# A four-layer graph network on one core: a reordered opening with dummy transposes, and a sign change moved from ScalarE to GpSimd

## The chip, the cores and the metric

The kernel runs on one core of a Trainium2 chip. The core has a matrix engine (TensorE, PE in the profile, with its weight loads shown apart as PEld), a vector engine (VectorE, DVE), a scalar engine (ScalarE, ACT), a general engine (GpSimd, POOL) and a queue engine that only starts transfers (SyncE, SP). Each engine works through its own instructions strictly in order; semaphores tie them together. The metric is the time of one execution on the device in microseconds; lower is better. Most repeats of this kernel agree within a few tenths of a per cent, with an occasional one above.

## What is computed

`x` holds 32 graphs of 512 nodes with 128 features; `adj` is one symmetric 0/1 matrix of 512x512 with a full diagonal, shared by all graphs. Four layers follow each other, each wrapped in a residual sum and a layer norm:

```python
x = _layernorm(x + _L0_gnn_ref(x, adj, W, b, a_src, a_dst))   # graph attention, leaky relu
x = _layernorm(x + _L1_gnn_ref(x, adj, W, a_src, a_dst))      # graph attention, elu
x = _layernorm(x + _L2_gnn_ref(x, adj, W, e, bias))           # weights by edge, diagonal apart
x = _layernorm(x + _L3_gnn_ref(x, adj, weight, bias))         # adj @ x + x, linear, L2 norm
# attention (layers 0 and 1):
h = x @ W;  e_src = h @ a_src;  e_dst = h @ a_dst
alpha = softmax(leaky_relu(e_src[:, None] + e_dst[None, :], 0.2) + mask(adj))
out = alpha @ h
# layer norm:
(x - mean(x)) / sqrt(var(x) + 1e-5)
```

All is float32. With these inputs all values of `e` are equal, so layer 2 is a mean over neighbours; the kernel tests that and two other properties of the inputs on the device and has a general path for when they fail. That path is not run here.

## The kernel before

Everything is unrolled. A graph's work is cut into named units ("pt0", "al0", "nrm2" and so on), each a few instructions on one engine, and a table gives every unit of every graph its place in one long list: `PLAN[name][graph]` for the work of the graphs, `STARTS[name]` for work done once. The list is sorted by these numbers and emitted in that order (L613 to L632), with buffers taken from fixed stocks when a unit first names a tile and returned after its last use. So the order on each engine is written out by hand (by an offline planner), nothing is scheduled at build time, and several graphs are always in flight.

Units of one graph in attention layer k (0 or 1): "ld" starts the transfer of x (L142, on SP); "pt" makes four 128x128 transposes (L149, PE), "xt" copies them out (L153, ACT); "pha/phb" multiply by the weight matrix extended by three attention columns (L167, PE); "exa/exb" take exponentials of those three columns (L171, ACT) into the array `exps`; "ha/hb" scale the projected features (L177, ACT), "pc" puts the scale in a last column (L192, POOL); "pr" spreads one exponential along a row by four transposes (L197, PE); "al" builds the unnormalised attention matrix with the mask `mt` in four instructions of 128x512 (L205, DVE); "poa/pob" multiply it with the features (L184, PE, 16 matmuls, 32 records in the profile). Then come division and bias (L188, L212, L217), activation, residual ("add", L235, POOL), "bn" statistics (L307, L309, DVE), and the norm. The statistics tile already carries epsilon. "ms" negates the mean (L313, ACT), "pw" takes the power -1/2 of the variance and multiplies the negated mean by it (L317, L318, POOL), and "nrm" applies scale and shift (L323, ACT). Layers 2 and 3 split x into two parts ("xh" L241 ACT, "xl" L245 POOL) for exact products with a 512x512 matrix (L252, PE), copy out (L256), and multiply by weights (L266, L267, L279); layer 3 has a row norm (L289 ACT, L293 and L294 POOL, L300 DVE). "st" writes the result (L328, SP).

Work done once. `first()` (L334) issues on the ACT queue the layer-0 weights W0, its two attention vectors, a quarter of `adj`, and the same three transfers of layer 1; on SP the other three quarters of `adj`; it builds the identity (POOL), fills constants, and clears the eight statistics tiles. In the list, six "ld" come first (places 0 to 5), then six "pt0"/"xt0", then "awt0" (the transpose of W0, L364, PE), "awc0" (its copy, L368, DVE), "e0" to "e3" (threshold of the four pieces of `adj`, L385, DVE), "awq0" and "aws0" (attention columns, L372 and L377 to L379), "am" (mask transposes, L390, PE), "m" (mask copies, L395 DVE and L397 ACT), "rest" (seven constant transfers, L358, SP), "deg" (node degrees, L412 and L413, DVE), "cva/cvd" (the matrices of layers 2 and 3, L401, L402 ACT and L407, L408 POOL), and the three input tests "lpp/lpd" (L418, L422), "dv" (L427, L428) and "de" (L432 to L434).

Of the kernel before, what the change touches and what calls it, by code (L numbers as in the profile page):

```python
# [18 lines left out]
P = 128  # L19
Q = 32  # L20
EPS = 1e-5
# [4 lines left out]
def kernel(  # L26
# [48 lines left out]
    an, em = square("an"), square("em")  # L75
    mt = square("mt")
# [9 lines left out]
    exps = const.tile([P, B * 2, NCH, 3], F32, name="exps")  # L86
# [34 lines left out]
    kind("sq", 30, "x1 x2 x3 x4 o0 o1 o2 o3 t t3 xb y2 y3 xt0 xt1 xt2 tr1 tr2", plain([P, N]))  # L121
# [4 lines left out]
    kind("st", 8, "st0 st1 st2 st3", plain([P, NCH, 9]))  # L126
# [28 lines left out]
    def columns(xt, c, blocked):  # L155

        if blocked:
            return xt.rearrange("p (a c i) -> p c a i", a=4, c=NCH)[:, c]
        return xt[:, c * P : (c + 1) * P]

    for k in range(2):
        for half, s in enumerate("ab"):

            @unit(f"ph{k}{s}", f"xt{k}", f"ph{k}{s}")
            def _(b, xt, p, k=k, half=half):
                for c in range(2):
                    nc.tensor.matmul(twos(p)[:, c, :FE], columns(xt, 2 * half + c, (b, f"td{k}") in planned), ATT[k], start=True, stop=True)  # L167

            @unit(f"ex{k}{s}", f"ph{k}{s}")
            def _(b, p, k=k, half=half):  # L170
                nc.scalar.activation(pair(exps[:, 2 * b + k], half), twos(p)[:, :, F:FE], AF.Exp)  # L171

            @unit(f"h{k}{s}", f"ph{k}{s}", f"h{k}")
            def _(b, p, h, k=k, half=half):
                for c in range(2):
                    pc = exps[:, 2 * b + k, 2 * half + c, 1:2]
                    nc.scalar.activation(h[:, 2 * half + c, :F], twos(p)[:, c, :F], AF.Identity, bias=pc if k else 0.0, scale=pc)  # L177
# [12 lines left out]
        @unit(f"pc{k}", f"h{k}")  # L190
        def _(b, h, k=k):
            nc.gpsimd.tensor_copy(h[:, :, F], exps[:, 2 * b + k, :, 1])  # L192

        @unit(f"pr{k}", f"pr{k}")
        def _(b, p, k=k):
            for c in range(NCH):
                nc.tensor.transpose(p[:, c * P : (c + 1) * P], exps[:, 2 * b + k, c, 0:1].to_broadcast([P, P]), ident)  # L197

        @unit(f"al{k}", f"pr{k}", f"al{k}")
        def _(b, p, al, k=k):  # L200
            attention(b, k, p, al)

    def attention(b, k, r, al):
        for j in range(NCH):
            nc.vector.scalar_tensor_tensor(al[:, j, :], r, exps[:, 2 * b + k, j, 2:3], mt[:, j, :], op0=ALU.max, op1=ALU.mult)  # L205
# [57 lines left out]
    def _(b, y, xt, p):  # L263
        for c in range(NCH):
            cols = slice(c * P, (c + 1) * P)
            nc.tensor.matmul(p[:, cols], y[:, cols], w21, start=True, stop=False)  # L266
            nc.tensor.matmul(p[:, cols], columns(xt, c, (b, "td2") in planned), w20, start=False, stop=True)  # L267
# [34 lines left out]
    for k in range(4):  # L302
# [8 lines left out]
        @unit(f"ms{k}", f"mv{k}")  # L311
        def _(b, mv):
            nc.scalar.activation(mv[:, :, 0], mv[:, :, 0], AF.Copy, scale=-1.0)  # L313

        @unit(f"pw{k}", f"mv{k}", f"rn{k}")
        def _(b, mv, rn):
            nc.gpsimd.tensor_tensor(rn[:, 0], mv[:, :, 1], mhalf, op=ALU.pow)  # L317
            nc.gpsimd.tensor_mul(rn[:, 1], mv[:, :, 0], rn[:, 0])  # L318

# [10 lines left out]
    for n in ("aw0", "aw1", "aq0", "aq1", "pm0", "pm1", "pm2", "pm3", "pflag"):  # L330
        KIND[n] = "ps"
    KIND["loops"], KIND["other"] = "sq", "al"

    def first():  # L334
        def attention_weights(k, w, a_src, a_dst):
            nc.scalar.dma_start(ATT[k][:, :F], w)
            for i, s in enumerate((a_src, a_dst)):
                nc.scalar.dma_start(acols[k][:, i : i + 1], bass.AP(tensor=s.tensor, offset=s.offset, ap=[[1, F], [1, 1]]))

        attention_weights(0, w0, asrc0, adst0)  # L340
        for c in range(NCH):
            (nc.scalar if c == 3 else nc.sync).dma_start(an[:, c, :], adj[c * P : (c + 1) * P, :])
# [4 lines left out]
        attention_weights(1, w1, asrc1, adst1)  # L347
        nc.gpsimd.tensor_scalar(nident, ident, -1.0, 1.0, op0=ALU.mult, op1=ALU.add)
        nc.gpsimd.memset(ones, 1.0)
        for st in FREE["st"]:  # L350
            nc.gpsimd.memset(st[:, :, 6:8], 0.0)
            nc.gpsimd.memset(st[:, :, 8], P * EPS)

# [55 lines left out]

    @unit("deg")  # L410
    def _(b):
        nc.vector.tensor_reduce(rdeg, em, axis=AX.X, op=ALU.add)  # L412
# [13 lines left out]
    def _(b, other):  # L426
        nc.vector.tensor_tensor(other, an, em, op=ALU.not_equal)  # L427
        nc.vector.tensor_reduce(doubts[:, 1:2], other.rearrange("p c f -> p (c f)"), axis=AX.X, op=ALU.max)  # L428
# [8 lines left out]
    def _(b):  # L437
        flat = exps.rearrange("p n c e -> p (n c e)")
# [12 lines left out]
    def _(b, p):  # L451
# [3 lines left out]
        "awt0": 13, "awc0": 16, "e0": 17, "rest": 19, "awq0": 21, "am0": 22, "e1": 24, "aws0": 25, "e2": 26,  # L455
        "awt1": 27, "am1": 28, "awc1": 29, "e3": 30, "deg": 32, "lpp": 33, "am2": 34, "am3": 37, "lpd": 42, "m2": 43,
        "awq1": 44, "m1": 46, "m0": 47, "cva2": 49, "m3": 50, "aws1": 52, "cva3": 55, "cvd2": 57, "cva0": 59,
        "cvd3": 60, "cva1": 61, "cvd0": 62, "dv": 63, "cvd1": 66, "de": 85, "out_d": 2297, "out_p": 2366,
        "out_c": 2370,
    }  # L460
    PLAN = {
        "ld": [5, 131, 168, 232, 184, 261, 1, 3, 4, 0, 2, 304, 298, 345, 513, 539, 787, 383, 665, 829, 904, 957, 1216,
            1245, 1067, 1349, 1154, 1578, 1434, 1696, 1791, 1819],
        "pt0": [18, 134, 169, 233, 195, 262, 7, 11, 15, 6, 9, 328, 422, 577, 624, 699, 793, 855, 799, 975, 1043, 959,
            1223, 1367, 1394, 1483, 1540, 1579, 1631, 1698, 1793, 1820],
        "xt0": [23, 136, 175, 235, 198, 266, 10, 14, 20, 8, 12, 340, 429, 582, 626, 704, 797, 866, 804, 985, 1052, 962,
            1229, 1371, 1400, 1491, 1543, 1586, 1637, 1705, 1797, 1829],
        "ph0a": [36, 140, 179, 241, 206, 270, 48, 56, 93, 65, 101, 350, 514, 597, 645, 731, 803, 872, 969, 990, 1090,
            1187, 1234, 1449, 1450, 1497, 1551, 1593, 1643, 1711, 1802, 1834],
        "ph0b": [31, 139, 182, 265, 203, 272, 45, 58, 91, 53, 51, 352, 523, 598, 641, 753, 805, 896, 973, 1031, 1113,  # L470
            1190, 1253, 1463, 1401, 1494, 1547, 1629, 1641, 1755, 1827, 1895],
        "ex0a": [38, 144, 185, 246, 208, 273, 67, 68, 96, 69, 104, 353, 518, 602, 650, 735, 806, 874, 974, 996, 1095,
            1192, 1246, 1454, 1452, 1503, 1554, 1600, 1651, 1718, 1805, 1837],
        "ex0b": [35, 141, 188, 269, 209, 281, 71, 73, 94, 74, 72, 361, 526, 603, 647, 766, 809, 900, 976, 1035, 1119,
            1199, 1257, 1468, 1410, 1505, 1552, 1639, 1644, 1765, 1831, 1900],
        "pc0": [39, 145, 190, 274, 211, 285, 75, 76, 98, 78, 105, 373, 531, 611, 652, 770, 815, 901, 979, 1042, 1122,
            1203, 1263, 1471, 1457, 1507, 1561, 1645, 1668, 1784, 1833, 1904],
        "pr0": [41, 146, 197, 276, 214, 290, 87, 90, 97, 95, 137, 399, 579, 655, 678, 772, 856, 922, 1029, 1099, 1158,
            1241, 1303, 1473, 1486, 1707, 1836, 1871, 1759, 1824, 1898, 1990],
        "h0a": [40, 148, 191, 279, 216, 287, 77, 79, 99, 83, 107, 384, 534, 616, 654, 774, 817, 905, 982, 1045, 1123,  # L480
            1205, 1267, 1479, 1462, 1509, 1562, 1647, 1669, 1785, 1835, 1905],
        "h0b": [64, 153, 194, 282, 218, 291, 80, 82, 100, 86, 108, 390, 537, 622, 660, 783, 820, 910, 986, 1050, 1127,
            1211, 1273, 1482, 1464, 1514, 1569, 1653, 1673, 1787, 1841, 1906],
        "al0": [54, 150, 213, 296, 230, 317, 92, 106, 113, 133, 200, 492, 583, 675, 769, 790, 869, 955, 1063, 1120,
            1188, 1282, 1315, 1650, 1516, 1714, 1866, 1903, 1762, 1826, 1921, 1996],
        "po0a": [81, 160, 222, 305, 248, 335, 103, 111, 126, 152, 215, 509, 620, 717, 782, 860, 907, 1008, 1075, 1147,
            1202, 1293, 1369, 1661, 1523, 1741, 1883, 1912, 1776, 1873, 1955, 2009],
        "po0b": [70, 163, 229, 313, 255, 342, 109, 115, 117, 207, 474, 499, 628, 737, 789, 865, 925, 1033, 1118, 1182,
            1212, 1314, 1387, 1667, 1533, 1732, 1877, 1917, 1783, 1902, 1970, 2056],
        "rs0a": [88, 164, 236, 316, 257, 364, 112, 123, 170, 172, 224, 515, 629, 722, 792, 868, 916, 1014, 1086, 1155,  # L490
            1222, 1299, 1377, 1670, 1531, 1752, 1891, 1920, 1788, 1879, 1971, 2022],
        "rs0b": [84, 171, 237, 332, 275, 357, 118, 122, 132, 228, 482, 508, 642, 759, 801, 878, 942, 1048, 1128, 1197,
            1221, 1325, 1398, 1679, 1548, 1739, 1885, 1928, 1799, 1909, 1979, 2069],
        "v0a": [89, 166, 245, 333, 283, 365, 119, 125, 173, 181, 226, 516, 637, 724, 796, 883, 923, 1015, 1088, 1162,
            1226, 1302, 1379, 1678, 1532, 1753, 1894, 1929, 1800, 1882, 1974, 2030],
# [454 lines left out]
```

## Time and profile before

| | us |
|---|---|
| median of three runs | 612.37 |
| lowest, highest | 612.05, 615.69 |
| the profiled execution | 614.38 |
| its span (first to last instruction in the profile) | 612.5 |
| first matmul record on PE starts at | 7.84 |
| PE, mean granted clock over the span | 0.985 |
| ACT, L313 (128x4), 128 times | 25.9 busy, 0.206 each |
| POOL, L317 / L318 (128x4), 128 times each | 1.042 / 0.212 each |
| POOL, L293 (128x4), 32 times | 0.228 each |
| DVE, L205 (128x512), 256 times | 173.4 busy, 0.738 each |
| ACT, L323 (128x128), 512 times | 209.4 busy, 0.488 each |

In the profile, a line such as "L184 PE MATMUL ps<-hp,al" names the source line, the engine, the operation and the tiles written and read. The instructions of an engine overlap a little, so the step from one to the next is shorter than the mean duration of one. A float32 matmul leaves two records on PE, a transpose one. "Idle before" is the time an engine stood still ahead of an instruction, with what ended it.

### The profile page before, as it was taken

What the parts mean: (1) busy time and instruction counts of PE and PEld (TensorE: products, weight loads), DVE (VectorE), ACT (ScalarE), POOL (GpSimd) and SP (SyncE); (2) the same over time, 40 slices, a digit from 0 to 9 for tenths busy, and PEclk for the clock granted to TensorE, in tenths of its full rate; (3) what the DMA queues carried; (4) which work ended last, traced back from release to release, by engine and by line L of the source; (5) the groups of instructions that cost most, each with busy time, mean ns of one, the idle gap of its engine ahead of it and who ended that gap; (6) DMA issues with size and microseconds to landing.
All of it is one profiled execution on the core that took longest, in us unless ns stands there. A gap on an engine that the chain in (4) does not pass through costs nothing.

```text
span 612.5 us, 13814 instructions
## 1 busy us (share of the span) xinstructions
PE 576.7 (94%) x4504; PEld 545.4 (89%) x4504; DVE 529.7 (86%) x1985; ACT 488.1 (80%) x1547; POOL 422.8 (69%) x580
## 2 busy tenths in 40 slices
PE   4898999999998999999999999999999999999881
PEld 4798998999998999989999999999999999998770
DVE  1998999787989999779989888799999999887864
ACT  3634777868889788786897989888885798999896
POOL 1422477586678776686768775868755786899885
PEclk9899999999999999999999999999999999999995
DMA  7001111000100111010201110010100001001003
GB/s 208 7 24 32 35 53 36 2 1 19 36 19 14 40 53 53 1 36 2 71 1 36 35 54 2 18 36 19 53 18 19 2 1 36 27 9 36 19 17 90
DMA packets 36316, 19.41 MB, mean 32 GB/s; under 512 B 1808, under 2 KB 35728, under 8 KB 36240
## 3 DMA queue, kind: packets, MB, share of 16 engines
q1 hardware_dynamic: 35232, 18.09, 10.3%
q8 instruction: 37, 0.61, 0.4%
q10 hardware_dynamic: 1008, 0.40, 0.2%
q14 instruction: 39, 0.32, 0.2%
HBM read 10.09 MB, written 8.39 MB: 30 GB/s over the span
## 4 chain that ended last, share of the span: by engine, by line
PE 68%; DVE 14%; ACT 8%; POOL 7%; issue 2%; DMA 1%; ACTq 0%; POOLq 0%; DVEq 0%
PE ps L184 30%; PE ps L252 12%; PE ps L167 8%; PE ps L149 5%; DVE al L205 5%; ACT sq L323 4%; PE ps L266 4%; PE ps L267 4%; PE ps L197 3%; PE ps L279 3%; DVE st L307 2%; POOL rn L317 2%; DVE sq L300 2%; POOL ss L294 1%; DVE sq L273 1%
## 5 line engine op out<-in xcount | busy, mean ns | idle before, releaser
L184 PE MATMUL ps<-hp,al 128*128 128x129 f32 x2048 | 246.1, 276 | 1.4 <-DVE al L205 1.1
L184 PEld LDWEIGHTS ps<-hp,al 128*128 128x128 f32 x2048 | 238.9, 192 | 3.7 <-DVE al L205 1.7
L323 ACT ACTIVATE sq<-sq,rn 128x128 f32<-128x128 f32 x512 | 209.4, 488 | 17.8 <-POOL rn L318 17.4
L205 DVE SCALAR_TENSOR_TENSOR al<-ps,exps,mt 128x512 f32<-128x512 f32 x256 | 173.4, 738 | 2.6 <-PE ps L197 2.5
L317 POOL TENSOR_TENSOR rn<-mv,mhalf 128x4 f32<-128x4 f32 x128 | 133.3, 1042 | 28.7 <-DVE mv L309 25.7
L307 DVE BATCH_NORM_STATS2 st<-sq 128x6 f32<-128x128 f32 x512 | 109.9, 276 | 12.4 <-POOL sq L235 12.3
L245 POOL TENSOR_TENSOR xr<-sq,xr 128x512 fp32r<-128x512 f32 x64 | 84.4, 1321 | 18.8 <-ACT xr L241 11.7
L177 ACT ACTIVATE hp<-ps,exps 128x128 f32<-128x128 f32 x256 | 89.3, 420 | 0.1
L153 ACT COPY sq<-ps 128x512 f32<-128x512 f32 x96 | 54.9, 582 | 28.6 <-PE ps L149 28.3
L167 PE MATMUL ps<-we,sq 128*128 128x131 f32 x512 | 71.5, 278 | 4.0 <-DVE al L205 2.5
L167 PEld LDWEIGHTS ps<-we,sq 128*128 128x128 f32 x512 | 64.2, 190 | 6.5 <-DVE al L205 2.7
L252 PE MATMUL ps<-off,xr 128*128 128x512 f32 x256 | 67.3, 405 | 1.1 <-DVE al L205 1.1
L252 PE MATMUL ps<-a3t,xr 128*128 128x512 f32 x256 | 66.6, 403 | 0.0
L235 POOL TENSOR_TENSOR sq<-sq,x 128x512 f32<-128x512 f32 x32 | 41.8, 1305 | 25.6 <-DVE sq L221 22.4
L260 POOL TENSOR_TENSOR sq<-sq,bias_b 128x512 f32<-128x512 f32 x32 | 41.0, 1283 | 21.2 <-ACT sq L323 19.2
L252 PEld LDWEIGHTS ps<-a3t,xr 128*128 128x128 f32 x256 | 46.3, 188 | 10.2 <-POOL xr L245 0.7
L252 PEld LDWEIGHTS ps<-off,xr 128*128 128x128 f32 x256 | 45.8, 188 | 10.3 <-DVE al L205 1.4
L266 PE MATMUL ps<-w,sq 128*128 128x128 f32 x256 | 49.8, 276 | 1.9 <-DVE al L205 1.8
L235 POOL TENSOR_TENSOR sq<-sq,sq 128x512 f32<-128x512 f32 x32 | 41.9, 1310 | 13.8 <-DVE rs L188 7.1
L267 PE MATMUL ps<-w,sq 128*128 128x128 f32 x256 | 49.5, 275 | 0.0
L313 ACT ACTIVATE mv<-mv 128x4 f32<-128x4 f32 x128 | 25.9, 206 | 29.3 <-DVE mv L309 21.2
L300 DVE SCALAR_TENSOR_TENSOR sq<-sq,ss,sq 128x128 f32<-128x128 f32 x128 | 42.3, 391 | 8.1 <-POOL ss L294 7.9
(78 smaller groups left out, 861.1 us busy)
## 6 DMA issues: line engine op xcount, KB each, us to landing
x<-in_x_dram SPq DMA_DIRECT2D x32, 256.0 KB, 2.9
out_dram<-sq SPq DMA_DIRECT2D x32, 256.0 KB, 2.2
an<-in_adj_dram SPq DMA_DIRECT2D x3, 256.0 KB, 3.9
an<-in_adj_dram ACTq DMA_DIRECT2D x1, 256.0 KB, 4.6
we<-in_L_gnn_W_dram ACTq DMA_DIRECT2D x2, 64.0 KB, 3.7
w<-in_L_gnn_W_dram SPq DMA_DIRECT2D x2, 64.0 KB, 3.4
bias_b<-in_L_gnn_bias_dram SPq DMA_DIRECT2D x2, 64.0 KB, 4.0
eb<-in_L_gnn_e_dram SPq DMA_DIRECT2D x1, 128.0 KB, 5.3
```

Source lines behind the costliest of these rows:

```text
L167: nc.tensor.matmul(twos(p)[:, c, :FE], columns(xt, 2 * half + c, (b, f"td{k}") in planned), ATT[k], start=True, stop=True)
L177: nc.scalar.activation(h[:, 2 * half + c, :F], twos(p)[:, c, :F], AF.Identity, bias=pc if k else 0.0, scale=pc)
L184: nc.tensor.matmul(twos(p)[:, c, : F + 1], al[:, j, rows], h[:, j, :], start=(j == 0), stop=(j == NCH - 1))
L205: nc.vector.scalar_tensor_tensor(al[:, j, :], r, exps[:, 2 * b + k, j, 2:3], mt[:, j, :], op0=ALU.max, op1=ALU.mult)
L235: nc.gpsimd.tensor_add(o, o, xk)
L245: nc.gpsimd.tensor_sub(xl, xk, xh.bitcast(F32))
L252: nc.tensor.matmul(p, part[:, j * P : (j + 1) * P], mat[:, j, :], start=(i + j == 0), stop=(i + j == NCH))
L266: nc.tensor.matmul(p[:, cols], y[:, cols], w21, start=True, stop=False)
L267: nc.tensor.matmul(p[:, cols], columns(xt, c, (b, "td2") in planned), w20, start=False, stop=True)
L307: nc.vector.bn_stats(st[:, c, :6], o[:, c * P : (c + 1) * P])
L317: nc.gpsimd.tensor_tensor(rn[:, 0], mv[:, :, 1], mhalf, op=ALU.pow)
L323: nc.scalar.activation(xo[:, c * P : (c + 1) * P], o[:, c * P : (c + 1) * P], AF.Identity, bias=rn[:, 1, c : c + 1], scale=rn[:, 0, c : c ...
```

## The change

The opening is rewritten, a sign moves, some once-only work moves, one array's layout changes, and the two place tables are replaced as a whole.

- `first()` now issues on the ACT queue one quarter of `adj` and the layer-0 weights, and nothing of layer 1. A tiny exponential follows on ScalarE. On SP, x of graph 0 comes first ("ld" at place 0), then three quarters of `adj` ("ja"), the layer-1 weights ("wb"), x of graphs 1 to 3, the seven constants ("rest"), and x of graphs 4 and 5.
- On PE, twelve transposes of the identity ("warm") stand first, eight more ("warm2") after the transposes of W0 and of graph 0.
- The degrees are summed on ScalarE ("dga", four activations of 128x512 with an accumulator) and inverted on VectorE. The test "dv" is one VectorE instruction with an accumulator, and it, "lpp" and "lpd" are placed later.
- "ms" is gone; "pw" has a third GpSimd instruction that multiplies its 128x4 result by -1.
- `exps` is stored as [graph and layer, 3, chunk], before [graph and layer, chunk, 3]. Six statistics tiles take the place of eight. The helper `columns` (which always took its second branch) is gone.

```diff
@@ names
-    exps = const.tile([P, B * 2, NCH, 3], F32, name="exps")
+    exps = const.tile([P, B * 2, 3, NCH], F32, name="exps")
-    kind("st", 8, "st0 st1 st2 st3", plain([P, NCH, 9]))
+    kind("st", 6, "st0 st1 st2 st3", plain([P, NCH, 9]))
@@ norm
-        @unit(f"ms{k}", f"mv{k}")
-        def _(b, mv):
-            nc.scalar.activation(mv[:, :, 0], mv[:, :, 0], AF.Copy, scale=-1.0)
-
         @unit(f"pw{k}", f"mv{k}", f"rn{k}")
         def _(b, mv, rn):
             nc.gpsimd.tensor_tensor(rn[:, 0], mv[:, :, 1], mhalf, op=ALU.pow)
             nc.gpsimd.tensor_mul(rn[:, 1], mv[:, :, 0], rn[:, 0])
+            nc.gpsimd.tensor_single_scalar(rn[:, 1], rn[:, 1], -1.0, op=ALU.mult)
@@ opening
+    def attention_weights(k, w, a_src, a_dst, eng):
+        eng.dma_start(ATT[k][:, :F], w)
+        for i, s in enumerate((a_src, a_dst)):
+            eng.dma_start(acols[k][:, i : i + 1], bass.AP(tensor=s.tensor, offset=s.offset, ap=[[1, F], [1, 1]]))
+    def adjacency(c, eng):
+        eng.dma_start(an[:, c, :], adj[c * P : (c + 1) * P, :])
     def first():
-        attention_weights(0, w0, asrc0, adst0)
-        for c in range(NCH):
-            (nc.scalar if c == 3 else nc.sync).dma_start(an[:, c, :], adj[c * P : (c + 1) * P, :])
+        adjacency(2, nc.scalar)
+        attention_weights(0, w0, asrc0, adst0, nc.scalar)
         make_identity(nc, ident)
...
-        attention_weights(1, w1, asrc1, adst1)
+        nc.scalar.activation(bad[:, 0:1], minus1, AF.Exp)
...
+    @unit("ja")
+    def _(b):
+        for c in (0, 1, 3):
+            adjacency(c, nc.sync)
+    @unit("wb")
+    def _(b):
+        attention_weights(1, w1, asrc1, adst1, nc.sync)
+    @unit("warm", "pf")
+    def _(b, p):
+        for i in range(12):
+            nc.tensor.transpose(p[:, :P], ident, ident)
+    @unit("warm2", "pf")
+    def _(b, p):
+        for i in range(8):
+            nc.tensor.transpose(p[:, :P], ident, ident)
@@ degrees and tests
+    @unit("dga", "junk")
+    def _(b, junk):
+        for c in range(NCH):
+            nc.scalar.activation(junk, em[:, c, :], AF.Copy, accum_out=rdeg[:, c : c + 1])
     @unit("deg")
     def _(b):
-        nc.vector.tensor_reduce(rdeg, em, axis=AX.X, op=ALU.add)
         nc.vector.reciprocal(rdeg, rdeg)
     @unit("dv", "other")
     def _(b, other):
-        nc.vector.tensor_tensor(other, an, em, op=ALU.not_equal)
-        nc.vector.tensor_reduce(doubts[:, 1:2], other.rearrange("p c f -> p (c f)"), axis=AX.X, op=ALU.max)
+        nc.vector.scalar_tensor_tensor(other, an, 1.0, em, op0=ALU.mult, op1=ALU.not_equal, accum_out=doubts[:, 1:2])
@@ places
     STARTS = {
-        "awt0": 13, "awc0": 16, "e0": 17, "rest": 19, "awq0": 21, "am0": 22, "e1": 24, "aws0": 25, "e2": 26,
-        "awt1": 27, "am1": 28, "awc1": 29, "e3": 30, "deg": 32, "lpp": 33, "am2": 34, "am3": 37, "lpd": 42, "m2": 43,
-        "awq1": 44, "m1": 46, "m0": 47, "cva2": 49, "m3": 50, "aws1": 52, "cva3": 55, "cvd2": 57, "cva0": 59,
-        "cvd3": 60, "cva1": 61, "cvd0": 62, "dv": 63, "cvd1": 66, "de": 85, "out_d": 2297, "out_p": 2366,
-        "out_c": 2370,
+        "ja": 1, "warm": 2, "wb": 3, "awt0": 4, "awc0": 6, "warm2": 7, "e2": 8, "e0": 12, "e1": 14, "rest": 15,
+        "awq0": 16, "am2": 17, "aws0": 18, "e3": 19, "am0": 20, "am1": 24, "am3": 29, "m3": 33, "awt1": 34, "m0": 35,
+        "m1": 37, "awc1": 40, "m2": 41, "awq1": 44, "cva2": 47, "cvd2": 54, "cva3": 57, "aws1": 61, "cvd3": 66,
+        "dga": 67, "de": 69, "deg": 78, "cva0": 91, "cva1": 92, "cvd0": 94, "cvd1": 97, "lpp": 256, "dv": 357,
+        "lpd": 416, "out_d": 2194, "out_p": 2224, "out_c": 2237,
     }
     PLAN = {
-        "ld": [5, 131, 168, 232, 184, 261, 1, 3, 4, 0, 2, 304, 298, 345, 513, 539, 787, 383, 665, 829, 904, 957, 1216,
+        "ld": [0, 9, 11, 13, 30, 100, 118, 177, 237, 295, 356, 410, 470, 521, 583, 645, 694, 746, 805, 866, 919, 985,
...
```

Before, the six graphs loaded first are numbers 9, 6, 10, 7, 8 and 0; after, they are 0 to 5, in order. All other rows of `PLAN` are replaced likewise. On PE the order after the change begins: twelve dummies, W0's transpose, four transposes of graph 0, eight dummies, the attention columns, eight mask transposes, the projection of graph 0 (8 records), four mask transposes, "pr" of graph 0, four mask transposes, the transposes of graphs 1, 2 and 3 with W1's between, the projections of graphs 1 and 3, the transposes of graph 4, "pr" of graph 1, the projection of graph 2, and then the first L184 units, of graph 0. On ScalarE the four sums of "dga" stand after the first two L177 of graph 1.

## The prediction, made before the run

> **What bounds the kernel now.** I read the page's busy table and slices first, then busy time by stage, then the chain of waits at the beginning, then the timeline there. Busy time and slices:
>
> ```profile
> PE 576.7 (94%) x4504; PEld 545.4 (89%) x4504; DVE 529.7 (86%) x1985; ACT 488.1 (80%) x1547; POOL 422.8 (69%) x580
> ...
> PE   4898999999998999999999999999999999999881
> ```
>
> TensorE is full except in the first slices and the last. By stage (microseconds, length, then busy time and instructions of PE, PEld, DVE, ACT, POOL, granted clock, DMA):
>
> ```profile
> 7.84:24.29 16.45, 13.31 (x86) 12.04 (x87) 10.73 (x23) 10.38 (x27) 5.92 (x12) 1.00 0.41 103
> 24.29:33.90 9.61, 8.69 (x60) 8.38 (x61) 8.39 (x16) 4.91 (x23) 2.41 (x6) 0.82 0.01 2
> 33.90:60.00 26.10, 24.39 (x215) 23.92 (x214) 23.70 (x71) 10.05 (x34) 7.84 (x11) 1.00 0.11 32
> 60.00:560.00 500.00, 495.15 (x3942) 471.72 (x3940) 451.71 (x1714) 417.78 (x1318) 364.85 (x476) 1.00 0.09 26
> ```
>
> The second line is the one with a clock below 1.00. The chain prices a record: L184 x16 takes 1.79, so 0.112 each at full pace. Then 86 records are 9.6 us of work, but lie in 16.45, after 7.84 with none: 14.7 of the first 24.29 us are lost. The next stage loses 9.61 - 60 x 0.112 = 2.9, the third 26.1 - 215 x 0.112 = 2.0. From 60 to 560, PE idles 4.85 of 500 us. So the beginning is the only large loss before the tail. Its chain of waits, in order of time (start, length, what):
>
> ```profile
> 1.24 4.15 DMA acols<-in_L_gnn_a_src_dram
> ...
> 5.40 3.97 DMA x<-in_x_dram
> ...
> 9.41 2.90 PE ps L149 x12
> 12.31 0.21 PE ps L364
> ...
> 19.69 0.69 DVE mt L395
> ...
> 24.29 5.47 PE ps L184 x32
> ```
>
> x is issued late: the SP queue, free at 2.14, issues the first x at 4.01, after the wait "L142 <- DMA we" of 1.8. Eight transfers are then under way and the ninth waits for an old one to land. Six graphs' transposes (L149) stand ahead of the one of W0 (L364). VectorE shows what that costs (start, length, engine, line):
>
> ```profile
> 12.56 0.29 DVE L368 COPY wt<-ps 128x128 f32<-128x128 f32 x1 [11.57 <-PE ps L364]
> 12.77 0.75 DVE L385 TENSOR_SCALAR em<-an 128x512 f32<-128x512 f32 x2
> ...
> 20.48 2.72 DVE L205 SCALAR_TENSOR_TENSOR al<-ps,exps,mt 128x512 f32<-128x512 f32 x4
> 23.12 2.28 DVE L427 TENSOR_TENSOR al<-an,em 128x2048 f32<-128x2048 f32 x1
> 25.43 2.29 DVE L428 TENSOR_REDUCE doubts<-al 128x1 f32<-128x2048 f32 x1
> ```
>
> VectorE waited 11.57 us for W0's transpose and thresholds the adjacency only then, though ScalarE's wait for a piece of it ended at 5.58. Then L427, L428 delay the next attention matrix (L205) to 30.58.
>
> **The change, the beginning.** Landing times of these transfers (minimum, median, maximum): x 3.7, 4.2, 4.9; adjacency 3.0, 4.2, 4.6; W 3.2, 3.7, 4.3; a vectors 2.8, 3.7, 4.6. First issues stand at 0.80 on SP and ACT, each taking some 0.42 to 0.46.
> - x of graph 0 is first on SP: lands by 0.8 + 3.7 to 4.2 = 4.5 to 5.0. W0, second on ACT (issued 1.24), lands near 4.9; the a vectors (issued 1.7 and 2.2) near 6; the last adjacency piece (SP, 2.1) near 6.3.
> - The identity is there at 1.37. Twelve dummy transposes at the cold 0.24 of L149 (12 in 2.90) end at 4.3, hidden by the wait for W0, free. Then W0's transpose and four of x, cold, to about 6.2. The second eight dummies stand in front of work: 0.9 at 0.112, 1.9 at 0.24; they end near 8.0.
> - VectorE copies W0's transpose at 5.3 (12.56 before) and thresholds three pieces by 6.7. The a-vector matmuls run at 8.1, L377 to L379 end at 8.8, the fourth threshold at 9.3. On TensorE follow 16 transposes of the mask, 8 projections and 4 of L197's kind, 28 x 0.112 = 3.1, with one wait for the exponentials: done at about 11.3. The mask copies on VectorE (2 x 0.65) and ScalarE (after two pairs of L177, 1.1) end by 12.9. The first attention matrix then stands at about 12.5 to 15.2 (20.48 to 23.2 before).
> - On SP, the W1 group (3 transfers) now comes before x of graph 1, and seven constants before x of graphs 4 and 5. Each waits for a slot of the eight: x1 goes near 5.4 and lands near 9.6, needed at 11.3; x4 goes near 10.7, lands near 14.5. TensorE is in order, so the graph-4 transposes hold graph 0's L184.
> - From 11.3 to the first L184 TensorE has 47 more records (5.2 us): start near 16.5, against 24.29. By then it has done 82 records against 86 (four fewer, 0.45). Net **7.3**, by bounds of the landings (0.6 either way) and the dummies 6 to 8.5.
>
> **Next stage.** Gone from VectorE are L412 (2.29), L428 (2.29), and, moved into the middle, L427 (2.28) and L422 (0.65). The degrees are four ScalarE sums over 128x512. Nearest rows: L153 128x512 0.58, L289 128x128 with its accumulator read 0.30 + 0.19 at a pitch of 0.29. So 4 x 0.57 to 0.77 = 2.3 to 3.1. Queued behind them on ScalarE are exponentials, transposed copies and L177 of graph 1; TensorE waits for that last L177, by my count of the queue (xt 0.5, mask casts 0.52, L177 pair 0.55 each) near 22. From 16.5 there are 44 records, 4.9, so 0.6 is lost before graph 1's L184 instead of 2.9. I take **2.0**; bounds 0 and 2.9. In the third stage I keep the 2.0 loss.
>
> **The rest.** 128 ScalarE instructions L313 (0.206 each, but a step of 0.10 to the next) go; 128 on POOL come. Nearest row L293, 128x4, 0.228; the dependent L293 to L294 step is 0.30 to 0.34. So 0.23 to 0.34 each, I take 0.27: 35 us on POOL, which idles 500 - 364.85 = 135 between 60 and 560. There it is hidden; were the cover gone, 35 us. In the tail the chain is largely POOL (L294 13.3%, L317 12.0% of its last 33 us); seven L317 start after 584. All seven on the path are 1.9, none is 0 (less 0.7 for L313 steps): I charge **1.0**. L427, with an accumulator now, and L422 land in a VectorE that idles 48 of those 500 us: 0 to 3.1, I take **0.5**. The exps layout moves no instruction and keeps every element count (L171 6 elements, L192 4): 0, hidden under TensorE. The final state has no other added work, but the order of all units is new.
>
> Sum: 7.3 + 2.0 - 1.0 - 0.5 = 7.8. The profiled execution took 614.38, its span 612.5, so 1.9 lie around it, and it is 2.0 above the median 612.37. Span 612.5 - 7.8 = 604.7; the median becomes **604.6**.
>
> [...] In this trace 26 transposes run from 7.84, spaced 0.24, and after only two small matmuls at 14.02 the next transposes are spaced 0.11 (4 in 0.64 including the last one's length). So a stream of transposes was enough to raise the pace (the granted clock reads 1.00 all through this stretch; the spacing is what shows it). [...] I go by the row.
>
> **Rivals.**
> 1. *The slow pace stays to the first long matmul run.* For it: no record before 14 runs fast, and PE's clock fell to 0.50 at 25 to 27 after a stage half idle. Against: the spacing at 14.24. Price 24 x 0.13 + 1.0 = 4.1: 608.7.
> 2. *The gain is given back by the new order.* Every unit after the beginning has a new place. PE idles 4.85 in the 500 us, 1.6 from 560 to 584 and 2.4 to 599; doubling all of it costs 8.8, eating the 7.8: 613. For it: VectorE is 451.7 of 500 busy, so few places are free. Against: VectorE's work does not grow there by more than 3.1.
> 3. *Slower: POOL's longer step decides the norm chain.* Each of 128 norms waits for POOL: ScalarE L323 waited for L318 30 times, 17.4 us. If the added 0.27 passes through to TensorE, the break-even is 7.8 + 1.0 over 0.27 = 33 of 128; half of them cost 17.3 - 1.0 = 16.3 more: 621. Against: TensorE's waits name POOL only 0.7 us (LDWEIGHTS after L245).
>
> **How the numbers follow.** Forecast 0.55 (own range 601 to 607.5), rival 1 0.15, rival 2 0.18, rival 3 0.12. One per cent, about what a measurement here tells from no change, is 606.2 and 618.5. Faster: nine tenths of the forecast (0.50) and a third of rival 1: 0.55. Slower: rival 3 and a little of rival 2: 0.14. Same: 0.31. The range runs from 599, the bounds 8.5 and 2.9 with the tail free and a little more, to 613: rivals 1 and 2 are in, rival 3 and a few hundredths at each end are out.
>
> **What would show it.** Right: x's first transposes before 6 us; the first attention matrix near 12.5; the first L184 between 15.5 and 18; the mask transposes spaced 0.11; PE idle between 60 and 560 still under 8. Wrong: mask transposes spaced 0.24 (rival 1); PE's waits grown in the middle, with VectorE as releaser (rival 2) or with POOL's rn in the chain of waits well above its 2% (rival 3); ScalarE's four sums as what ends TensorE's wait for graph 1.

## The result and the profile after

| | before | after |
|---|---|---|
| median, us | 613.30 (4 runs, 612.05 to 615.69) | 620.39 (4 runs, 619.96 to 622.48) |
| profiled execution / its span | 614.38 / 612.5 | 619.96 / 618.3 |

The ratio is 1.0111, interval 1.0081 to 1.0142: slower by 1.1%. The forecast was 604.6, with 599 to 613 as its range; the time lies where rival 3 put it (621).

The busy table of after, whose first figures are the busy us and the share of the span, and TensorE's row of the 40 slices:

```profile
PE 580.4 (94%) x4524; PEld 545.7 (88%) x4524; DVE 524.0 (85%) x1984; ACT 476.4 (77%) x1428; POOL 460.1 (74%) x704
...
PE   8899999999999899989999999999999999999970
```

The first slice rises from 4 tenths to 8 (the dummies count as busy) and the fourth from 8 to 9; some slices of the middle fall to 8. POOL has 37.3 us more than before, ACT 11.7 less. Busy time by stage, with columns as in the forecast's table:

```profile
7.84:24.29 16.45, 13.36 (x114) 12.89 (x113) 9.45 (x26) 12.86 (x42) 2.52 (x8) 1.00 0.37 102
24.29:33.90 9.61, 9.61 (x89) 9.61 (x88) 9.57 (x30) 2.79 (x7) 4.48 (x7) 1.00 0.11 31
33.90:60.00 26.10, 25.72 (x228) 25.09 (x227) 24.14 (x78) 20.38 (x67) 12.71 (x25) 1.00 0.14 41
60.00:560.00 500.00, 489.48 (x3855) 462.45 (x3854) 443.56 (x1672) 396.29 (x1185) 393.77 (x577) 1.00 0.09 25
```

The two stages with large losses before now have 114 and 89 records instead of 86 and 60, at a granted clock of 1.00. But TensorE idles 10.5 of the long 500 us, where it idled 4.85, and VectorE's work in that stage fell along with it (451.71 to 443.56). Counting the records that TensorE has begun shows both sides (the 20 dummies left out, 0.112 us each by the forecast's price):

| TensorE's records begun by | before | after | after is |
|---|---|---|---|
| 24.29 us | 86 | 117 | 3.5 ahead |
| 60 us | 359 | 429 | 7.8 ahead |
| 80 us | 536 | 606 | 7.8 ahead |
| 560 us | 4299 | 4281 | 2.0 behind |
| the end of the span | 612.5 us | 618.3 us | 5.8 behind |

So the opening won most of the 9.3 that was forecast. The middle, which the forecast charged 0.5, lost 9.8; the tail, charged 1.0, lost 3.8. The groups by line say where (busy us and mean ns of one, then idle time of that engine just ahead of them and what ended it):

```profile
L314 ACT ACTIVATE sq<-sq,rn 128x128 f32<-128x128 f32 x512 | 210.9, 486 | 87.8 <-POOL rn L309 83.6
...
L301 DVE BATCH_NORM_STATS2 st<-sq 128x6 f32<-128x128 f32 x512 | 110.0, 276 | 24.9 <-POOL sq L229 24.7
...
L294 DVE SCALAR_TENSOR_TENSOR sq<-sq,ss,sq 128x128 f32<-128x128 f32 x128 | 40.9, 381 | 16.3 <-POOL ss L288 14.9
```

L309 is the new sign instruction. ScalarE stood 83.6 us for it ahead of the norms (L314, the former L323), against 17.4 for L318 before. Two waits of VectorE for POOL's *other* work doubled too: 24.7 for the residual sum (12.3 before) and 14.9 for the row norm's power (7.9). One such place in the timeline, engine by engine (start, length, engine, line):

```profile
269.46 0.20 POOL L308 TENSOR_TENSOR rn<-mv,rn 128x4 f32<-128x4 f32 x1
269.75 0.59 POOL L309 TENSOR_SCALAR rn<-rn 128x4 f32<-128x4 f32 x1
```

```profile
270.38 1.65 ACT L314 ACTIVATE sq<-sq,rn 128x128 f32<-128x128 f32 x4 [0.85 <-POOL rn L309]
271.93 0.57 ACT L153 COPY sq<-ps 128x512 f32<-128x512 f32 x1
```

```profile
272.55 1.16 PE L161 MATMUL ps<-we,sq 128*128 128x131 f32 x8 [1.97 <-ACT sq L153]
```

The norm waits for POOL, the copy L153 waits behind the norm on ScalarE, and TensorE waits 1.97 us for the copy. TensorE's own row names ScalarE, and POOL appears two steps up the chain. Over the whole span these are the largest waits of its matmuls (us in total, how many, the longest):

```profile
PE ps L161 <- ACT sq L153: 5.5, 6, 2.0
PE ps L246 <- POOL xr L239: 3.6, 3, 1.9
```

Before, its matmuls waited 0.5 for that copy, and for POOL's split (L239, the former L245) not at all.

### The profile page after: what moved, and what is told of

Read it like the earlier page. It is cut to its first block, busy times and chain, and to the rows that moved or that the text cites. A ratio compares the mean times of both kernels' runs of the same rounds, so it can differ in the third digit from the quotient of the medians.

```text
span 618.3 us, 13781 instructions
## 1 busy us (share of the span) xinstructions
PE 580.4 (94%) x4524; PEld 545.7 (88%) x4524; DVE 524.0 (85%) x1984; ACT 476.4 (77%) x1428; POOL 460.1 (74%) x704
## 5 line engine op out<-in xcount | busy, mean ns | idle before, releaser
L314 ACT ACTIVATE sq<-sq,rn 128x128 f32<-128x128 f32 x512 | 210.9, 486 | 87.8 <-POOL rn L309 83.6
L178 PE MATMUL ps<-hp,al 128*128 128x129 f32 x2048 | 246.5, 274 | 2.4 <-DVE al L199 2.1
L178 PEld LDWEIGHTS ps<-hp,al 128*128 128x128 f32 x2048 | 238.3, 191 | 4.2 <-issue 2.3
L199 DVE SCALAR_TENSOR_TENSOR al<-ps,exps,mt 128x512 f32<-128x512 f32 x256 | 173.4, 739 | 1.5 <-PE ps L191 1.5
L307 POOL TENSOR_TENSOR rn<-mv,mhalf 128x4 f32<-128x4 f32 x128 | 137.4, 1074 | 45.0 <-DVE mv L303 27.7
L301 DVE BATCH_NORM_STATS2 st<-sq 128x6 f32<-128x128 f32 x512 | 110.0, 276 | 24.9 <-POOL sq L229 24.7
L171 ACT ACTIVATE hp<-ps,exps 128x128 f32<-128x128 f32 x256 | 87.7, 419 | 0.2
L239 POOL TENSOR_TENSOR xr<-sq,xr 128x512 fp32r<-128x512 f32 x64 | 83.4, 1305 | 2.4 <-ACT xr L235 2.4
L161 PE MATMUL ps<-we,sq 128*128 128x131 f32 x512 | 73.0, 278 | 5.7 <-ACT sq L153 5.5
L161 PEld LDWEIGHTS ps<-we,sq 128*128 128x128 f32 x512 | 64.9, 190 | 8.5 <-ACT sq L153 7.4
L153 ACT COPY sq<-ps 128x512 f32<-128x512 f32 x96 | 54.3, 584 | 8.5 <-PE ps L149 8.3
L294 DVE SCALAR_TENSOR_TENSOR sq<-sq,ss,sq 128x128 f32<-128x128 f32 x128 | 40.9, 381 | 16.3 <-POOL ss L288 14.9
L246 PEld LDWEIGHTS ps<-off,xr 128*128 128x128 f32 x256 | 45.9, 188 | 9.3 <-DVE al L199 0.3
L303 DVE BATCH_NORM_AGGREGATE mv<-st 128x2 f32<-128x9 f32 x512 | 49.1, 157 | 0.0
```

The source lines that it names most:

```text
L153: nc.scalar.copy(xt, p)
L161: nc.tensor.matmul(twos(p)[:, c, :FE], xt[:, (2 * half + c) * P : (2 * half + c + 1) * P], ATT[k], start=True, stop=True)
L178: nc.tensor.matmul(twos(p)[:, c, : F + 1], al[:, j, rows], h[:, j, :], start=(j == 0), stop=(j == NCH - 1))
L239: nc.gpsimd.tensor_sub(xl, xk, xh.bitcast(F32))
L246: nc.tensor.matmul(p, part[:, j * P : (j + 1) * P], mat[:, j, :], start=(i + j == 0), stop=(i + j == NCH))
L301: nc.vector.bn_stats(st[:, c, :6], o[:, c * P : (c + 1) * P])
```

## Experiments

Ratios are to the kernel before, with their intervals. The diffs of a1, a2, a4 and b2 to b4 are to the kernel after, those of b1 and c1 to c3 to a2, that of a3 to before.

**a1: without the sign.** The multiplication by -1 is left out.

```diff
-            nc.gpsimd.tensor_single_scalar(rn[:, 1], rn[:, 1], -1.0, op=ALU.mult)
```

> The changed kernel without the third GpSimd instruction of each norm (128 of them); the multiplication by -1 is left out and nothing takes its place, so the norm adds its mean term. Everything else, order included, stays. Up to 80 us the changed kernel has lost 10.1 us of TensorE time against 19.9 before; from there to the end it loses 36.5 against 22.6. Theory sign (the longer GpSimd step holds up ScalarE's norm, L314, and with it TensorE): those 13.9 us go, time about 606 to 609, ScalarE's wait for GpSimd ahead of L314 falls from 83.6 to below 40 us. Theory order (the new place tables are worse by themselves): 617 to 620, TensorE's idle time between 60 and 560 stays near 10 us.

Measured: 604.41, ratio 0.9847 (0.9821 to 0.9873). Without these 128 instructions the time is that of the forecast (604.6).

**a2: the sign back on ScalarE,** in the new plan.

```diff
+        @unit(f"ms{k}", f"mv{k}")
+        def _(b, mv):
+            nc.scalar.activation(mv[:, :, 0], mv[:, :, 0], AF.Copy, scale=-1.0)
...
-            nc.gpsimd.tensor_single_scalar(rn[:, 1], rn[:, 1], -1.0, op=ALU.mult)
...
+    PLAN.update({f"ms{k}": [t - 0.5 for t in PLAN[f"pw{k}"]] for k in range(4)})
```

> The changed kernel with the negation of the mean back on ScalarE, one instruction of 128x4 ahead of each unit that takes the power, as before; GpSimd has two instructions a norm again. Theory sign: most of the 13.9 us go, less some 0.1 us of ScalarE step for each of 128 instructions of which few are on the path: 607 to 611. Theory order: 617 to 621.

Measured: 604.78, ratio 0.9855 (0.9833 to 0.9876). This version beats both kernels. Against a1 it has 128 negations more on ScalarE, 26.3 us of instructions (busy time 491.5 against 476.6), and takes the same time within the intervals: the negation was free where it had been. Its long stage and its waits on POOL:

```profile
60.00:560.00 500.00, 497.70 (x3929) 472.55 (x3927) 452.23 (x1722) 418.98 (x1323) 372.65 (x480) 1.00 0.09 26
```

```profile
ACT sq L317 <- POOL rn L312: 29.0, 37, 1.5
...
DVE st L301 <- POOL sq L229: 13.7, 12, 2.5
...
DVE sq L294 <- POOL ss L288: 12.0, 9, 2.7
```

TensorE idles 2.3 of the 500 us. The columns of the waits are us in total, how many, and the longest: the norm's wait falls from 83.6 to 29.0, that for the residual sum from 24.7 to 13.7 (12.3 before), that for the row norm's power from 14.9 to 12.0 (7.9 before).

**a3: only the sign moved,** in the kernel before.

```diff
-        @unit(f"ms{k}", f"mv{k}")
-        def _(b, mv):
-            nc.scalar.activation(mv[:, :, 0], mv[:, :, 0], AF.Copy, scale=-1.0)
...
+            nc.gpsimd.tensor_single_scalar(rn[:, 1], rn[:, 1], -1.0, op=ALU.mult)
```

> The kernel before with only the sign moved: the ScalarE negation is gone, GpSimd multiplies by -1 as a third instruction. Order and opening are those of before. Theory sign: slower by 6 to 14 us, 619 to 627, with TensorE's idle time between 60 and 560 up from 4.85 to 10 or more. Theory order: within 3 us of the kernel before, 611 to 616.

Measured: 629.28, ratio 1.0259 (1.0238 to 1.0279): 16.2 us over its neighbour in the same comparison (613.06). In the new plan the same step costs 620.39 - 604.78 = 15.6. So the new order of the units neither made this cost nor softened it, and the rest of the change by itself is worth 604.78 - 613.06 = -8.3.

**a4: one dummy in place of twelve, one in place of eight.**

```diff
-        for i in range(12):
+        for i in range(1):
...
-        for i in range(8):
+        for i in range(1):
```

> The changed kernel with one dummy transpose in the place of twelve and one in the place of eight. If the dummies warm the clock as read from the spacing before (0.24 to 0.11 after some 5 us of transposes): the 16 mask transposes and 8 projections run at 0.24, the first L178 starts 0 to 3 us later than 20.3, time 0 to 3 us longer, 620 to 624. If transposes do not warm it: the mask transposes of the changed kernel were warm for another reason, no difference or 1 to 2 us shorter, 618 to 620. Both theories of the later loss expect that loss unchanged.

Measured: 622.04, ratio 1.0148 (1.0125 to 1.0170); the interval overlaps that of after. The mask transposes and the projections after them were spaced 0.22 here (8 in 1.95, twice), up to 11.1 us. That is not the dummies' absence alone, since kernels with all twenty dummies spaced their mask transposes at 0.11 in some executions (8 in 1.07 in a1) and at 0.22 in others (8 in 1.95 in a2 as well). Records begun by 80 us, dummies aside, are 589 here, 593 in a2 and 606 in after. What the dummies are worth, 0 to 1.7 us, is not settled by these runs.

The next four take the sign apart. Two theories of its price: *queue*, POOL is occupied for longer and its other work comes late; *chain*, the norm itself waits for one more dependent step.

**b1: the same work, read by nobody.** a2 with a third POOL instruction of the same form, whose result goes to a tile of its own.

```diff
+    aside = const.tile([P, NCH], F32, name="aside")
...
+            nc.gpsimd.tensor_single_scalar(aside, rn[:, 1], -1.0, op=ALU.mult)
```

> The sign on ScalarE (604.8), plus on GpSimd after the two instructions of each norm a third one of the same form as the changed kernel's, on the same operand, whose result goes to a tile that nobody reads. So GpSimd's queue is as long as in the changed kernel, but the norm of the same graph need not wait for it. Theory queue (GpSimd's time delays whatever stands behind in its order, the sums and splits of 1.3 us): 616 to 621, nearly all of the 15.6 us is back. Theory latency (only the 0.3 us between the statistics and the norm count): 605 to 608.

Measured: 617.29, ratio 1.0055 (1.0030 to 1.0080): 12.5 of the 15.6 us are back although no norm waits for the added instruction. Its waits show which work it delays:

```profile
ACT sq L319 <- POOL rn L313: 40.1, 50, 1.6
...
DVE st L302 <- POOL sq L230: 23.8, 23, 3.0
...
DVE sq L295 <- POOL ss L289: 15.1, 12, 3.2
```

```profile
PE ps L162 <- ACT sq L154: 4.5, 7, 1.3
PE ps L247 <- POOL xr L240: 3.6, 3, 2.0
```

VectorE's two waits for POOL are those of after (24.7 and 14.9) and not those of a2, and TensorE's waits for the copy and the split are near those of after too (5.5 and 3.6; in a2 the second is 1.1 and the first is not listed). The norm's wait is 40.1, well below the 83.6 of after. So most of the price is that POOL does this work at all, and a large wait of ScalarE ahead of the norms is largely not what costs. One part of the 12.5 was not taken apart from the queue: VectorE's own instructions are longer in the two runs with the busier POOL. Its busy time is 523.9 here and 524.0 in after, 520.3 in a2; its leaky relu (L215 in after and a2) takes 767, 773 and 709 ns.

**b2: the negation ahead of the product.** After, with the mean negated on POOL first and multiplied then; two of the three results are still needed by the norm.

```diff
+            nc.gpsimd.tensor_single_scalar(rn[:, 1], mv[:, :, 0], -1.0, op=ALU.mult)
...
-            nc.gpsimd.tensor_mul(rn[:, 1], mv[:, :, 0], rn[:, 0])
-            nc.gpsimd.tensor_single_scalar(rn[:, 1], rn[:, 1], -1.0, op=ALU.mult)
+            nc.gpsimd.tensor_mul(rn[:, 1], rn[:, 1], rn[:, 0])
```

> The changed kernel with the three GpSimd instructions in another order: the mean times -1, then the power, then the product. The third no longer waits for the second's result, so the step of 0.1 us in front of it should go; the busy time of 0.23 stays. Theory that the dependent step matters (31.8 busy and 11.2 idle for 128): 4 us faster than the changed kernel, 615 to 617. Theory that only the instruction's presence counts: 618 to 621.

Measured: 616.63, ratio 1.0048 (1.0027 to 1.0069), 3.8 below after and as b1 within the intervals. The same three instructions in another order cost less, though the two ratio intervals nearly touch (after's begins at 1.0081). This does not tell the two theories apart, since POOL's queue became shorter as well: by the medians of the trace the negation in front lengthens it by 0.19, the one behind the product in after by 0.33, and VectorE's wait for the residual sum is 18.3, between a2's 13.7 and after's 24.7.

**b3: the norms up to eight places later on ScalarE,** with the sign on POOL, so that ScalarE does other work in place of waiting.

```diff
+    readers = {0: ("pt1", "add1"), 1: ("pt2", "xb", "xh2", "xl2"), 2: ("xh3", "xl3", "rr"), 3: ("st",)}
+    for k, names in readers.items():
+        PLAN[f"nrm{k}"] = [min([t + 8] + [PLAN[n][b] - 0.5 for n in names]) for b, t in enumerate(PLAN[f"nrm{k}"])]
```

> The changed kernel with each norm unit (L314) placed up to 8 places later, never past the first unit that reads its result; GpSimd's work is unchanged. If ScalarE standing in order behind GpSimd is how the time is lost (83.6 us of waiting ahead of L314, with copies for TensorE queued behind), some of it comes back: 610 to 616 and that wait falls below 60. If the norm's own result is what others wait for, later makes it worse: 621 to 628.

Measured: 630.69, ratio 1.0285 (1.0257 to 1.0314), 10.3 worse than after. The wait named by the profile did shrink:

```profile
ACT exps L165 <- PE ps L161: 56.4, 38, 5.4
...
ACT sq L250 <- PE ps L246: 25.2, 19, 4.3
...
ACT sq L314 <- POOL rn L309: 22.5, 25, 3.6
```

The norm now waits 22.5 instead of 83.6, and ScalarE waits for TensorE instead (56.4 and 25.2, in after 22.6 and 3.2); that the work fed by the norm comes later would explain it. Removing the largest wait in the list of an engine that is not the bound made the kernel slower.

**b4: the sign on VectorE,** one more 128x4 instruction behind the statistics.

```diff
+            nc.vector.tensor_single_scalar(mv[:, :, 0], mv[:, :, 0], -1.0, op=ALU.mult)
...
-            nc.gpsimd.tensor_single_scalar(rn[:, 1], rn[:, 1], -1.0, op=ALU.mult)
```

> The changed kernel with the mean negated on VectorE, one 128x4 instruction behind the statistics, and two instructions a norm on GpSimd. A small VectorE instruction steps by 0.06 to 0.08 us, 128 of them 8 to 10 us of an engine that idles 56 of 500 in the changed kernel. If the cost is special to GpSimd (step 0.34): 605 to 609. If any added step in the norm chain costs the same per 0.1 us: 604.8 plus a quarter of 15.6, 607 to 611.

Measured: 630.56, ratio 1.0278 (1.0248 to 1.0307), 25.8 over a2. The timeline of one place:

```profile
206.04 0.39 DVE L303 BATCH_NORM_AGGREGATE mv<-st 128x2 f32<-128x9 f32 x4
206.46 0.17 DVE L304 TENSOR_SCALAR mv<-mv 128x4 f32<-128x4 f32 x1
206.54 0.60 DVE L267 SCALAR_TENSOR_TENSOR sq<-ps,rdeg,sq 128x128 f32<-128x128 f32 x2
```

In the timeline of after (269.56 to 274.71), the instruction that follows the four aggregations starts 0.30 behind the first of them (273.76 to 274.06). Here it is 0.50 (206.04 to 206.54), 0.20 more, as by the medians of all places. That 128 x 0.20 = 25.6 is the size of the loss is partly chance: VectorE's busy time rose by 40.8 (520.3 in a2, 561.1 here), since the new instruction takes 0.25 in the mean and other groups grew beside it (L294 from 40.5 to 45.9). Why they grew is not shown. The same sign costs 26 us there, 16 on POOL, nothing on ScalarE.

The last three are about the opening, and are all a2 with one change.

**c1: another PSUM bank for one tile.** The forecast had the first attention sum (L178, the former L184) at 16.5; it came at 20.33. These are TensorE's last records of the opening of after, and VectorE's two attention matrices:

```profile
16.25 0.66 PE L149 MATMUL ps<-ident,x 128*128 128x128 f32 x4 [1.00 <-DMA x<-in_x_dram]
16.75 0.60 PE L191 MATMUL ps<-ident,exps 128*128 128x128 f32 x4
17.18 1.06 PE L161 MATMUL ps<-we,sq 128*128 128x131 f32 x8
20.33 0.91 PE L178 MATMUL ps<-hp,al 128*128 128x129 f32 x6 [2.09 <-DVE al L199]
```

```profile
13.24 2.72 DVE L199 SCALAR_TENSOR_TENSOR al<-ps,exps,mt 128x512 f32<-128x512 f32 x4
...
17.46 2.73 DVE L199 SCALAR_TENSOR_TENSOR al<-ps,exps,mt 128x512 f32<-128x512 f32 x4 [1.31 <-PE ps L191]
```

The matrix that graph 0's sum reads ends at 15.96, yet the sum starts as the *second* L199, graph 1's, ends. The sum's result tile was given the bank that holds graph 1's row of exponentials (L191 at 16.75), which that L199 reads. The change:

```diff
-                    home[b, t] = FREE[KIND[t]].popleft()
+                    take = FREE[KIND[t]].pop if (b, t) == (0, "po0a") else FREE[KIND[t]].popleft
+                    home[b, t] = take()
```

> a2_sign_on_scalar with one change: the first half of graph 0's attention sum goes to the other PSUM bank, the one that graph 1's projections used, not the one that holds graph 1's row of exponentials. If the bank held the first attention sum up (in a2 L178 waited 2.09 us for L199 of graph 1 and began at 20.53, though graph 0's own L199 ended at 16.8), its first 8 records go once ScalarE's L171 has read the other bank, near 18.1, and the rest still near 20.5: 8 x 0.112 = 0.9 us better at most, near 604. If VectorE's L199 of graph 0 or something else set it, the first L178 stays at 20.5 and the time at 604.8. Either way within what can be told in time; the start of L178 tells them apart.

Measured: 602.47 (601.83 to 602.84), ratio 0.9812 (0.9780 to 0.9844). Every run lies below every run of a2 (603.67 to 605.25), on another chip; the ratio intervals overlap. The trace:

```profile
17.38 1.95 PE L178 MATMUL ps<-hp,al 128*128 128x129 f32 x16
19.54 2.05 PE L178 MATMUL ps<-hp,al 128*128 128x129 f32 x16 [0.21 <-DVE al L199]
```

The sum begins at 17.38, straight behind L161; the second half still waits for the old bank. So the bank was the wait. My size was low: half of a sum is 8 matmuls but 16 records, 1.8 us. TensorE's records begun by 80 us, dummies aside, are 631, against 593 in a2: 4.3 us. Of the difference, the records that now run during the old wait are 1.8; another part is that the granted clock fell to 0.50 for 3.4 us behind the wait in a2 and stayed at 1.00 here, and graph 1's L199 began 0.9 earlier (16.76 against 17.66). The edit also shifts which banks later tiles are given; what that is worth is not shown. This version has the lowest median of all.

**c2: the degrees back on VectorE.**

```diff
-            nc.scalar.activation(junk, em[:, c, :], AF.Copy, accum_out=rdeg[:, c : c + 1])
...
+        nc.vector.tensor_reduce(rdeg, em, axis=AX.X, op=ALU.add)
         nc.vector.reciprocal(rdeg, rdeg)
```

> a2_sign_on_scalar with the degrees back on VectorE: one sum over 128x2048 (2.29 us in the kernel before) instead of ScalarE's four sums (2.9 us at 17.9 to 20.9). If VectorE's time is paid in full, as the 25.6 us of b4_sign_on_vector were, 604.8 + 2.3 = 607.1. If ScalarE's four sums held graph 1's L171 up, as I forecast might be, part of that comes back: 604.8 to 606. If VectorE's early waits (3.7 us at 12.7, 2.9 at 24.1) cover it, 604.8.

Measured: 605.58, ratio 0.9868 (0.9841 to 0.9895), 0.8 over a2: neither the full price of 2.3 nor none can be excluded.

**c3: x of graph 0 behind the adjacency.** Its place in the list goes from 0 to 2.

> a2_sign_on_scalar with x of graph 0 issued behind the three adjacency pieces instead of first. If x first is what the opening's gain rests on, x's transposes wait from 5.4 to about 6.6 (three issues of some 0.42 later) and the mask's transposes come 1 us earlier: TensorE's first 80 us lose 0 to 1.2 more, 604.8 to 606. If the adjacency is what the opening waits for, 603.8 to 604.8, and loading x first is worth nothing or less.

Measured: 604.96, ratio 0.9865 (0.9830 to 0.9899): as a2. The transposes of x began at 7.05 (5.29 in a2) and the first L178 at 21.52 (20.53), but the clock stayed at 1.00 behind it. That x goes first shows no gain in time that these runs can tell.

## Why the prediction was wrong

**The step that failed** is in "The rest": that the sign's 35 us are *hidden* in the 135 us that POOL idles, and that only the tail pays, 1.0. POOL's busy time rose by about what was said (460.1 - 423.2 in a2 = 36.9). But 15.6 us of it came through to the end, 0.122 of each of the 128.
- *The idle time was no reserve.* POOL idles because it waits for VectorE's statistics and ScalarE's exponentials (25.7 and 35.5 us before), then has several short jobs at once that others wait for. b1 shows it: an instruction that nobody reads delays the residual sums and row norms behind it, and costs 12.5.
- *I looked at the wrong row.* "TensorE's waits name POOL only 0.7 us" was my reason against rival 3. POOL works mostly through ScalarE and VectorE, which had stood 17.4 + 12.3 + 7.9 us for it before; those rows were on the page and I weighed one of them. In after they are 83.6 + 24.7 + 14.9, and TensorE's own wait for POOL's split is 3.6.
- *The size of the step was low as well.* I took 0.27, within 0.23 to 0.34. In a2 the POOL instruction behind L312 starts 0.13 after it (264.00, 264.13); in after, L308 starts at 261.88, L309 at 262.17, and where L309 takes its common 0.23 the next one follows it by 0.20 (262.26 to 262.46 in b1). In these rows that is 0.29 + 0.20 - 0.13 = 0.36. By the medians over all norms (0.29 + 0.19 - 0.15) it is 0.33, or 42 us of the queue, of which a little over a third was paid.

**Rival 3 held,** at 621 against 620.4. Its mechanism was half right: I had it as the norm chain alone, while the larger part is POOL's queue, with what VectorE lost beside it (12.5, b1), and the dependent step is the smaller (3.1 by difference). Its price by "half of 128 at 0.27" was a guess that met the sum of the two.

**The removal from ScalarE** I priced at 0.7 in the tail; a1 against a2 shows no more. A busy ScalarE (81% of a2's span) had room for 128 negations: most ran beside POOL's power or ahead of it (L307 at 263.30 while L311 ran from 262.90 to 263.92 in a2) and 115 of the 128 ended before the power did. POOL's product waited for the rest only 4.3 us in all, 11 times.

**The opening came near in sum, by another course.** I forecast 7.3 + 2.0 = 9.3 by 33.9 us; it stood at 3.5 by 24.29, at 58 x 0.112 = 6.5 by 33.9, and at 7.8 by 60. The attention matrix came at 13.24 to 15.96 (forecast 12.5 to 15.2). The first L178 came 3.8 us late, from two things: x of graph 4 landed near 16.2 (I had 14.5), and TensorE, in order, put the row of graph 1 behind it; and the bank, which I had not looked at, tied graph 0's sum to graph 1's matrix (c1). The rest was then won behind it, where VectorE no longer had L412, L427 and L428 between attention matrices. The order and the once-only work together gave 8.3 (a2), against the 7.8 + 1.0 of my sum without the tail's term for the sign. That these are so near is partly luck: in a2 the opening stood at only 57 x 0.112 = 6.4 by 60, and part of the rest is TensorE idling 2.3 instead of 4.85 in the long stage, which I had charged 0.5. So rival 2 fell: the new order gives nothing back. Two readings of the trace of before were off, without weight in the sum: four graphs' transposes stood ahead of W0's, not six, and 25 transposes ran before the pace rose, not 26, most of them spaced 0.21.

**The dummies, and rival 1.** That a stream of transposes is enough to raise the pace was read from one stretch of before. In a1 nothing but transposes had run on TensorE when these came:

```profile
1.42 2.82 PE L358 MATMUL ps<-ident 128*128 128x128 f32 x12 [1.42 <-POOL ident masks.py:199]
5.18 0.33 PE L375 MATMUL ps<-ident,we 128*128 128x128 f32 x1 [0.93 <-DMA we<-in_L_gnn_W_dram]
5.35 0.60 PE L149 MATMUL ps<-ident,x 128*128 128x128 f32 x4
```

The first twelve are spaced 0.22, the four at 5.35 are spaced 0.11: the pace rose with transposes alone, as the forecast had taken it from the trace of before. The records of the granted clock agree with the spacing: the first, at 1.00, begins at 14.18 in before and at 8.77 in after, where the spacing changes from 0.21 to 0.11 (ahead of its first record the view shows 1.00 as well). But the dummies did not fix the moment. By the spacing the pace rose between 4.2 and 5.4 in a1 and b4, near 8.7 in after and c1, near 9.9 in b2, between 10 and 11 in a2, b1, b3, c2 and c3, all with the same twenty dummies; what sets it is not shown. In a2 the eight mask transposes were slow (8 in 1.95) and the pace rose among the projections behind them (8 in 1.40), as rival 1 has it; but its price of 4.1 does not show: by 80 us a2 had begun 593 records, dummies aside, and a1, where the pace rose first, 594.

## What to carry to other kernels

Idle time of an engine that passes short jobs between others was not room here (36.9 us of work, put on an engine that idled 135 of 500, cost 15.6): before moving work onto it, add up every wait for that engine, on all engines that feed the bound, and see what would stand behind the new work in its queue. Move such a step to where its input is already there and its result is not yet needed, even onto a busier engine (the sign cost nothing on ScalarE, busy for 81% of a2's span). Read the buffer numbers where a start comes late: a result bank that another graph still reads is a wait which the data's own dependencies don't show (in c1 the sum begins at 17.38, with the shared bank at 20.53 in a2).

## What the runs showed of the hardware

- A multiplication of 128x4 by a constant on POOL mostly takes 0.23, but up to 0.80 when VectorE's L215 or L223 (128x512, all operands in SBUF) runs beside it. In after, L309 took 0.80 during L215, and 0.59 in the place shown first, during L223 (269.56 to 270.25):

```profile
262.17 0.80 POOL L309 TENSOR_SCALAR rn<-rn 128x4 f32<-128x4 f32 x1
```

```profile
262.20 0.68 DVE L215 SCALAR_TENSOR_TENSOR sq<-sq 128x512 f32<-128x512 f32 x1
```

  Of the 128 in after, five took over 0.30 (0.59 to 0.80), all beside L215 or L223. But six that ran beside L294 (128x128, which reads two tiles from SBUF) took 0.23 to 0.24. Over all 128 it is small: the mean is 248 ns and the median 230, so 128 x 0.018 = 2.3 us.
- The granted clock fell to 0.50 for 3.41 us, shortly after TensorE's wait ahead of the first attention sums, in before (24.4 to 27.8), a2 (20.8 to 24.2), a1, a3, a4, b1, b3 and c2, and not in after, b2, b4, c1 and c3. In a2 the 32 records behind the wait took 5.45 us, in c3 3.81 behind the same wait of 2.09. This is 1.6 us between two executions with the same wait, so single openings should not be compared to a finer measure. The clock records of before and after hold three falls to 0.50, and each begins a whole number of 3.41 us behind the first record at 1.00: in before, from 14.18, three times (24.42) and 171 times (597.86); in after, from 8.77, 175 times (606.10). Counted on in these steps, the two waits ahead of the first sums in before (1.37 and 0.32, from 21.9 to 24.29) lie between the marks at 21.01 and 24.42; in after the mark at 19.01 cuts the wait of 2.09 (18.24 to 20.33) in two, and no fall follows. How much waiting between two marks it takes is not settled here.
